# A decoder layer on one core: the first score maximum ahead of the root, next tokens normalized a slot ahead, cross keys at the slot's end, cross output ahead of the key sums

## The chip, the core and the metric

The kernel runs on one core of a Trainium2 chip. Its engines are TensorE (PE in the profile; PEld is its weight loads), VectorE (DVE), ScalarE (ACT), GpSimd (POOL) and SyncE (SP), which issues most of the transfers. Each engine takes its instructions in order, and waits at an instruction until the semaphores it names have been reached. The metric is device time in microseconds, the median of the runs. Before the change it is 855.12 us over 3 runs (855.03 to 855.3).

## What is computed

A pre-norm decoder layer in fp32 over 16 rows of 128 tokens with 256 features: self attention with 16 heads of 64, cross attention with 16 heads of 16 on a context of the same size under a mask that is the same for all rows, and a dense mixture of 8 experts whose sum is scaled per token.

```python
x = x + self_attention(layernorm(x))        # softmax(QK'/8) V, W_O, biases
x = x + cross_attention(layernorm(x), ctx)  # softmax(mask(QK'/4)) V, Wo, biases
x = x + moe(layernorm(x))                   # sum_e gelu(x w1_e + b1_e) w2_e + b2_e, scaled by norm_g

def self_attention(x):
    scores = einsum('bqhk,bshk->bhqs', Q, K) / sqrt(64)
    return einsum('bqhk,hdk->bqd', einsum('bhqs,bshk->bqhk', softmax(scores), V), W_O) + b_O
```

## The kernel before, in words

The program has two parts. The attention part handles one row of 128 tokens after the other, and the expert part follows it over all tokens. The change touches only the attention part, which takes roughly the first 450 us.

The attention part is a software pipeline of 16 slots. Slot s holds the self attention of row s, the cross scores of row s-1, the cross output of row s-2 and the last normalization of row s-3. It also makes queries, keys and values of later rows, two rows at a time, by a scheme with seven products in place of eight: `paired_steps` for queries (names `q...`) and keys (`k...`), and `paired_values` (names `v...`).

The order of instructions is written out by hand. Each step of a slot has a name, and the table `DUE` (L55) gives every name a due time in us from the slot's start. `slot` (L1027) puts the steps into a heap with the key `EXTRA + s * SLOT + due` (`when`, L307), and `run_slots` pops them in that order; each engine's queue has the order in which its instructions were popped. The due times are sort keys and nothing else: no instruction waits for a clock. `FIRST_DUE`, `SECOND_DUE` and `LAST_DUE` replace some times in slots 0, 1, 14 and 15. Names that end in `e` or that name a read-out (`vu0`, `qc1`, `at2T`, ...) are the copies or additions by which ScalarE or VectorE take a result out of PSUM; their due times are given apart from the matmuls'.

The steps that the text needs, with the engines in brackets:

- `S0`, `S1` (PE): self scores of heads 0 to 7 and 8 to 15 (`self_scores`), each into one of two score tiles (`ps_sc`, two banks of PSUM each).
- `max0`, `max1` (DVE, 128x1024): their negated maxima; `ex0a`, `ex0b`, `ex1a`, `ex1b` (ACT): four exponentials each; `r..` (DVE): reciprocals of the sums; `mul..` (POOL): scaling. With a `c` ahead (`cmax0`, `cex0a`, ...) the same for the cross scores.
- `T1a1`, `T1a2`, `T1b1`, `T1b2` (PE): four transposes each of the self probabilities; `T2..` of the cross probabilities of row s-2. Their read-outs (`T2b1e`, ...) are copies of 128x512: on ACT for `T1a`, `T1b` and `T2a`, on DVE for `T2b`.
- `q1x`, `q1y`, `q2x`, `q2y`, and the same with `k` and `v` (PE): products of the seven-product scheme. `..1x` and `..2x` work in one PSUM tile, `..1y` and `..2y` in a second. The first tile is last read by `qc00` (ACT). The second is read by `qu2`, `qu3`, `qc1` and `qc0` (DVE), and likewise for `k` and `v`.
- `root`, `xn`, `xn3` (DVE): inverse root of the variances and normalization (`normalize_outputs`). `xn1`, `LN1`, `LN1c` (DVE, PE, ACT): normalization and transposes of two new rows (`self_norm_transposed`, odd slots to 11, and slot 0). `LNx`, `LNxc`: the same for the cross queries' row; `LN3`, `LN3c` for the experts.
- `CQ`, `CS`, `CV`, `CO` (PE): cross queries, cross scores (into both score tiles), cross values, cross output. `ck`, `cke`, `cke2`: cross keys and their four read-outs on ACT. `cvr`, `cvre`: cross value rows.
- `msk0`, `msk1` (DVE): the mask. `SVa`, `SVb`, `atT0`, `atT1`: self values and their read-outs. `SO`, `xsSO`: self output.

All matmul results but the scores share the pool `ps_mm`, which has four tiles of one PSUM bank:

```python
ps_mm = tc.tile_pool(name="ps_mm", bufs=4, space=PSUM, side="right")
ps_sc = tc.tile_pool(name="ps_sc", bufs=2, space=PSUM)
```

A matmul that opens a tile waits for the last reader of the tile that was in that bank before.

Of the kernel before, what the change touches and what calls it, by code (L numbers as in the profile page):

```python
# [30 lines left out]
GB = 2  # L31
NG = B // GB
# [17 lines left out]
NROW = 528  # L50


SLOT = 26.98
EXTRA = 7.86
DUE = dict(  # L55
    S0=0.0, S1=1.0, T2a1=2.05, T2a2=2.49, T2a1e=2.69, ck=2.92, T2a2e=3.19, max0=3.47, v1x=3.79,
    cke=3.99, vu0=4.3, cke2=4.4, max1=4.61, v1y=4.66, q1x=5.52, ex0a=5.54, vu1=6.08, q1y=6.42,
    vu2=6.76, qu0=6.91, vu3=7.24, r0a=7.32, v2x=7.32, mul0a=7.39, vc00=7.4, ex0b=7.41, qu1=7.63,
    v2y=7.77, qu2=8.06, qu3=8.49, LNx=8.6, q2x=8.64, vc1=8.84, q2y=9.09, LNxc=9.1, ex1a=9.13,
    vc0=9.19, r0b=9.53, mul0b=9.81, qc1=10.19, cvr=10.21, qc00=10.51, qc0=10.54, r1a=10.98,  # L60
    T2b1=11.23, mul1a=11.26, cvre=11.31, ex1b=11.66, T2b2=11.66, T2b1e=11.86, CQ=12.1,
    T2b2e=12.46, T1a1=12.97, q2T=13.17, T1a2=13.4, r1b=13.51, xn1=13.6, T1a1e=13.6, mul1b=13.79,
    CS=13.93, st0=14.0, mid=14.0, late=14.0, T1a2e=14.1, ab1=14.9, CV=14.97, msk0=15.08,
    LN3=16.07, at2T=16.27, T1b1=16.29, LN3c=16.49, msk1=16.61, T1b2=16.73, T1b1e=16.93,
    LN1=17.16, T1b2e=17.43, SVa=17.47, cmax0=17.8, LN1c=17.93, SVb=18.38, tf=18.93, mid2=18.93,
    atT0=18.94, late2=18.94, cex0a=19.12, k1x=19.43, atT1=19.54, cmax1=20.14, k1y=20.33,
    cex0b=20.49, SO=21.23, cr0a=21.28, cmul0a=21.56, ku0=21.86, cr0b=22.14, cex1a=22.36,
    cmul0b=22.58, ku1=22.58, ku2=23.01, ku3=23.44, cex1b=23.74, cr1a=23.94, st1=24.0,
    cmul1a=24.3, k2x=24.68, xsSO=24.88, k2y=25.12, bn=25.28, kc00=25.32, cr1b=25.78, CO=26.03,
    cmul1b=26.06, kc1=26.22, kc0=26.57, xsCO=27.09, bn3=27.5, root=28.09, xn=34.27, ab2=34.3,  # L70
    xn3=37.78,
)


FIRST_DUE = dict(
    fk0=-11.4, fq0=-9.5, fk0e=-9.4, fq0e=-7.7, fk1=-7.2, norm1=-7.0, S0=-5.4, fk1e=-5.3,
    fq1=-4.4, max0=-4.0, cross=-3.0, ex0a=-2.7, fLN=-2.65, fq1e=-2.6, fv0=-2.3, fLNc=-1.4,
    r0a=-1.32, ex0b=-1.3, mul0a=-1.2, S1=-0.6, fv0e=0.1, r0b=0.15, mul0b=0.2, fab0=0.25,
    fab1=0.3, max1=0.4, fv1=0.41, ex1a=1.65, early0=1.7, early1=1.75, cvr=2.22, fv1e=3.0,
    r1a=3.1, mul1a=3.2, early2=3.3, early3=3.35, ex1b=3.6, q0=3.96, cvre=5.0, r1b=5.1,  # L80
    mul1b=5.2, q0e=5.3, early=5.4, k0=6.57, ke0=8.56, ws0=8.7, v0=9.18, xn1=10.44, T1a1=10.9,
    ve0=11.1, T1a2=11.34, T1a1e=11.54, T1b1=11.77, T1a2e=12.14, T1b2=12.21, LN1=12.64,
    T1b1e=12.74, LN1c=13.06, T1b2e=13.34, w0q=13.6, w0k=13.7, SVa=14.25, SVb=15.15, atT0=15.42,
    q1=17.2, atT1=17.21, wv0=17.3, q1e=17.6, k1=18.0, w1q=18.1, tf=18.2, SO=19.16, ke1=19.6,
    ws1=19.7, w1k=20.0, xsSO=22.81, bn=23.22, v1=23.47, root=24.79, xn=25.0, ck=25.2, ve1=25.39,
    q1x=26.9, cke=26.9, cke2=26.91, qu0=26.95, q1y=27.8, qu1=28.2, ab2=28.44, ab1=28.5,
    k1x=28.7, qu2=28.8, k1y=28.9, qu3=29.2, ku0=29.3, ku1=29.85, ku2=30.0, ku3=30.1, q2x=30.5,
    q2y=30.95, qc00=31.0, qc1=32.0, qc0=32.5, k2x=32.8, kc00=33.3, k2y=33.4, kc1=34.5, kc0=34.9,
# [2 lines left out]
SECOND_DUE = dict(wv1=4.7, st0=11.9, st1=12.46, st2=16.3, tf=19.6, st3=24.0)  # L91

LAST_DUE = {
    14: dict(root=30.48, xn=33.0),
    15: dict(
        max0=1.2, max1=2.35, ex0a=3.3, cke=4.6, cke2=4.65, r0a=5.2, mul0a=5.4, vu0=5.9, ex0b=6.0,
        LNx=7.24, qu1=7.4, cvr=7.46, LNxc=7.6, ex1a=8.0, r0b=8.3, T2b1=8.33, mul0b=8.5,
        T2b2=8.77, T2b1e=8.85, CQ=9.2, T2b2e=9.3, cvre=9.5, ex1b=9.6, r1a=10.0, T1a1=10.1,
        mul1a=10.11, q2T=10.25, T1a2=10.55, CS=11.0, r1b=11.75, mul1b=11.85, CV=12.1,
        LN3=13.05, T1b1=13.3, T1b2=13.75,  # L100
    ),
}

# [11 lines left out]
def decoder_layer(  # L115
# [53 lines left out]
    def psum_mm(name):  # L169
        return ps_mm.tile([P, 512], F32, tag="mm", name=name)  # L170
# [51 lines left out]
    def context(g):  # L222
        c = work.tile([P, KD, GT], F32, tag="ctx", name=f"ctx{g}")
        nc.sync.dma_start(out=c, in_=ctxT[g])
        return c

    contexts = {0: context(0)}
# [55 lines left out]
    def urgent():  # L283

        return tc.high_priority()
# [5 lines left out]
    def at(name, f, *a):  # L291


        if now[0] is None:
            f(*a)
        else:
            heapq.heappush(events, (when(name), next(count), now[0], f, a))

    def due(name, f, *a):

        if now[0] is None:
            with urgent():
                f(*a)
        else:
            at(name, f, *a)

    def when(name):  # L307
# [3 lines left out]
        if s == 1 and name in SECOND_DUE:  # L311
            return EXTRA + SLOT + SECOND_DUE[name]
        d = LAST_DUE[s] if s in LAST_DUE and name in LAST_DUE[s] else DUE
        return EXTRA + s * SLOT + d[name]

# [446 lines left out]
    def cross_keys(b):  # L762
        kT = work.tile([P, C2, 2, T], F32, tag="k2T", name="k2T")
        g, i = b // GB, b % GB
        mm = psum_mm("mm_k2")[:, : C2 * T].rearrange("p (m t) -> p m t", m=C2)
        for m in range(C2):
            for k in range(KD):
                nc.tensor.matmul(
                    mm[:, m, :],
                    wx[:, 1, k, m * P : (m + 1) * P],  # L770
                    contexts[g][:, k, i * T : (i + 1) * T],
                    start=(k == 0),
                    stop=(k == KD - 1),
                )


        def out(m):
            for e in range(2):
                nc.scalar.activation(
                    kT[:, m, e, :],  # L780
                    mm[:, m, :],
                    AF.Identity,
                    bias=bkp[:, e, m : m + 1],
                    scale=par[:, e : e + 1],
                )

        due("cke", out, 0)
        due("cke2", out, 1)
        entry["k2T", b] = kT

    def cross_value_rows(b):
        g, i = b // GB, b % GB
        mm = psum_mm("mm_v2")
        for k in range(KD):
            nc.tensor.matmul(
                mm[:, :D],
                contexts[g][:, k, i * T : (i + 1) * T],
                wx_vo[:, 0, k, :],
                start=(k == 0),
                stop=(k == KD - 1),  # L800
            )
        due(
            "cvre",
            nc.scalar.copy,
            v2s[g % 2][:, i].rearrange("p (e w) -> p e w", e=2)[:, :, :D].rearrange(
                "p e (r t) -> p e r t", t=32
            )[:, :, :, :DH2],
            mm[:, :D].rearrange("p (r e d) -> p e r d", e=2, d=DH2),
        )
        if i == GB - 1 and g + 2 < NG:  # L810
            contexts[g + 2] = context(g + 2)

    def cross_queries(b):
        xnT2 = entry.pop(("xnT2", b))
# [212 lines left out]
    def slot(s):  # L1027


        for half in range(2):  # L1030
            at(f"S{half}", self_scores, s, half)
            at(f"SV{'ab'[half]}", self_values, s, half)
            for n in range(2):
                at(f"T1{'ab'[half]}{n + 1}", self_transposed, s, half, n)
                if s >= 2:
                    at(f"T2{'ab'[half]}{n + 1}", cross_transposed, s - 2, half, n)
        at("SO", self_output, s)
        at("cvr", cross_value_rows, s)
        at("ck", cross_keys, s)
        normalize_outputs(s, s - 2 if s >= 2 else None)  # L1040
        if s >= 1:
            at("LNx", cross_norm, s - 1)
            at("CQ", cross_queries, s - 1)
            at("CS", cross_scores, s - 1)
            at("CS", cross_softmax, s - 1)
        if s >= 2:
            at("CV", cross_values, s - 2)
            at("CO", cross_output, s - 2)
        if s >= 3:
            at("LN3", expert_norm, s - 3)  # L1050
        bs = [2, 3] if s == 0 else [s + 3, s + 4] if s % 2 and s + 4 < B else []
# [3 lines left out]
        if bs:  # L1055
            at("LN1", self_norm_transposed, bs)
        b0 = s + 2 - s % 2
# [18 lines left out]
        if s >= B - 2:  # L1076
            at("S0", load_w1, s - (B - 2), we1)
        for n, (s1, name, out) in enumerate(PRE_STEPS):
# [466 lines left out]
```

## Time and profile before

| | |
|---|---|
| Median of the runs | 855.12 us |
| The profiled execution's own time | 856.78 us |
| Its span, first to last instruction | 855.0 us |
| Granted TensorE clock | 0.997 |
| PE, PEld busy | 99%, 84% |
| DVE, ACT, POOL busy | 75%, 56%, 19% |

Each row of a timeline has the start in us, the duration, the engine, the line, the operation, `out<-in` by the program's names, shapes, how many instructions were merged, and in brackets the idle time ahead of it with what ended it. fp32 matmuls appear as two passes each. Passes overlap, so busy time says little, and the distance from start to start says how fast TensorE goes on: 0.110 us for a pass with 128 columns, 0.216 for 256, 0.43 for 512.

The starts of slots (first score matmul, `sc<-kT,qT` at L706, from the chain of waits): slot 1 49.32, slot 2 73.69, slot 3 100.90, slot 4 128.34, slot 5 155.22, slot 6 182.66, slot 7 209.91, slot 8 237.23, slot 9 264.11, slot 10 291.43, slot 11 318.31, slot 12 345.63, slot 13 372.52, slot 14 399.40, slot 15 424.94. The chain merges rows, so that some of these starts lie up to 0.07 us behind the first matmul.

### The profile page before, as it was taken

The numbers are of one execution on the slowest core, as the hardware profiler recorded it, in microseconds if no ns is written. First come the engines' busy times: TensorE is split into PE (matmuls) and PEld (weight loads), VectorE is DVE, ScalarE is ACT, GpSimd is POOL, SyncE is SP. The second block draws the span as 40 slices with busy tenths as digits, with TensorE's granted clock in tenths as the row PEclk, the third lists the DMA queues.
The fourth block names the chain that finished last, engine by engine and source line by source line (L and its number), as shares of the span: only waits on it lengthen the run. The fifth ranks groups of instructions, "written<-read, shape, count | busy, mean of one in ns | idle before, by whom it ended". The sixth has DMA issues, their size and how long they took to land.

```text
span 855.0 us, 16389 instructions
## 1 busy us (share of the span) xinstructions
PE 846.0 (99%) x5934; PEld 721.8 (84%) x5934; DVE 642.2 (75%) x1694; ACT 474.6 (56%) x1723; POOL 164.7 (19%) x180
## 2 busy tenths in 40 slices
PE   8999999999999999999999999999999999999997
PEld 7899889888889889898775468888888888888886
DVE  4888998899888889888677497686557755676565
ACT  3567687776868668776685523343334333343332
POOL 4133242433423343332432000000000000000000
PEclk9999999999999999999999999999999999999999
DMA  8500000000000000001151100000000000000000
GB/s 238 148 13 2 2 14 2 15 1 2 13 2 14 1 2 14 2 2 51 56 196 46 50 1 0 1 13 13 1 0 1 26 1 0 1 13 13 2 0 26
DMA packets 18321, 21.32 MB, mean 25 GB/s; under 512 B 9584, under 2 KB 13696, under 8 KB 17600
## 3 DMA queue, kind: packets, MB, share of 16 engines
q1 hardware_dynamic: 17728, 19.93, 7.4%
q8 instruction: 47, 0.77, 0.4%
q0 software_dynamic: 368, 0.30, 0.2%
q14 instruction: 34, 0.28, 0.1%
q10 hardware_dynamic: 144, 0.04, 0.0%
HBM read 18.16 MB, written 2.10 MB: 24 GB/s over the span
## 4 chain that ended last, share of the span: by engine, by line
PE 93%; DVE 3%; ACT 2%; DMA 1%; issue 0%; POOLq 0%; DVEq 0%; SPq 0%; ACTq 0%
PE y L1279 20%; PE mm_qk L565 10%; PE tr_p L442 6%; PE mm_o L751 6%; PE he L1279 6%; PE hf L1279 6%; PE ha L1279 6%; PE mm_v L656 5%; PE sc L706 4%; PE po L731 3%; PE mm_h L1017 3%; PE hb L1279 3%; PE mm_qk L500 2%; PE y L1192 2%; PE po L880 2%; PE sc L841 2%
## 5 line engine op out<-in xcount | busy, mean ns | idle before, releaser
L412 ACT ACTIVATE cpr<-sc,nmax 128x128 f32<-128x128 f32 x256 | 90.5, 402 | 17.5 <-DVE nmax L406 14.0
L412 ACT ACTIVATE pr<-sc,nmax 128x128 f32<-128x128 f32 x256 | 93.0, 410 | 2.7 <-DVE nmax L406 2.7
L427 POOL TENSOR_TENSOR cpr<-cpr,rinv 128x512 f32<-128x512 f32 x64 | 65.5, 1040 | 126.4 <-DVE rinv L423 126.3
L1308 ACT ACTIVATE h<-u,colv 128x256 f32<-128x256 f32 x56 | 28.4, 508 | 99.4 <-DVE u L1295 97.5
L427 POOL TENSOR_TENSOR pr<-pr,rinv 128x512 f32<-128x512 f32 x64 | 67.1, 1049 | 62.8 <-DVE rinv L423 59.7
L406 DVE TENSOR_REDUCE nmax<-sc 128x8 f32<-128x1024 f32 x64 | 76.4, 1215 | 0.2 <-PE sc L706 0.2
L1309 DVE TENSOR_TENSOR c<-u,hf 128x256 f32<-128x256 f32 x56 | 23.5, 419 | 68.3 <-PE hf L1279 68.1
L1387 POOL TENSOR_TENSOR yT<-y,yu 128x256 f32<-128x256 f32 x1 | 0.7, 722 | 377.9 <-ACT y L1386 377.9
L1292 ACT COPY u<-ha 128x256 f32<-128x256 f32 x56 | 20.8, 372 | 83.5 <-PE ha L1279 83.5
L1279 PE MATMUL hf<-xt,w 128*128 128x256 f32 x224 | 66.7, 379 | 0.0
L1279 PE MATMUL ha<-xnT,w 128*128 128x256 f32 x224 | 66.6, 379 | 0.0
L1279 PE MATMUL y<-t,w 128*128 128x256 f32 x224 | 66.6, 380 | 0.0
L412 ACT ACTIVATION_READ_ACCUMULATOR pr<-sc,nmax 128x1 f32 x256 | 63.7, 249 | 0.0
L412 ACT ACTIVATION_READ_ACCUMULATOR cpr<-sc,nmax 128x1 f32 x256 | 61.9, 242 | 0.0
L751 PE MATMUL mm_o<-wo,atT 128*128 128x256 f32 x256 | 58.1, 380 | 0.3 <-DVE atT L324 0.3
L1279 PE MATMUL y<-h,w 128*128 128x256 f32 x224 | 57.6, 379 | 0.0
L751 PEld LDWEIGHTS mm_o<-wo,atT 128*128 128x128 f32 x256 | 47.6, 190 | 7.4 <-issue 1.0
L1279 PEld LDWEIGHTS ha<-xnT,w 128*128 128x128 f32 x224 | 42.6, 190 | 7.1 <-issue 1.2
L1279 PEld LDWEIGHTS hf<-xt,w 128*128 128x128 f32 x224 | 42.5, 190 | 5.9 <-DVE u L1294 0.2
L1279 PEld LDWEIGHTS y<-h,w 128*128 128x128 f32 x224 | 42.6, 190 | 5.8
L1279 PEld LDWEIGHTS y<-t,w 128*128 128x128 f32 x224 | 41.9, 190 | 6.2 <-issue 0.8
L395 POOL TENSOR_TENSOR xs<-xs,rowv 128x256 f32<-128x256 f32 x32 | 23.3, 740 | 115.2 <-DVE xn L382 115.2
(253 smaller groups left out, 2115.3 us busy)
## 6 DMA issues: line engine op xcount, KB each, us to landing
w<-in_w SPq DMA_DIRECT2D x8, 1024.0 KB, 5.2
ctx<-in_ctxT SPq DMA_DIRECT2D x8, 256.0 KB, 2.5
out_x<-ot SPq DMA_DIRECT2D x8, 256.0 KB, 2.1
xs<-in_x SPq DMA_DIRECT2D x3, 512.0 KB, 5.8
wk<-in_wk SPq DMA_DIRECT2D x2, 512.0 KB, 7.2
wq<-in_wq SPq DMA_DIRECT2D x2, 512.0 KB, 7.8
wv<-in_wv SPq DMA_DIRECT2D x2, 512.0 KB, 9.7
wo<-in_wo SPq DMA_DIRECT2D x1, 1024.0 KB, 7.7
```

Of the source, the lines that this page charges most:

```text
L406: nc.vector.tensor_reduce(w["nmax"], sc, AX.X, ALU.max, negate=True)
L412: nc.scalar.activation(w["pr"][:, i, :], sc[:, i, :], AF.Exp, bias=w["nmax"][:, i : i + 1], scale=1.0, accum_out=sums[:, j : j + 1],)
L427: nc.gpsimd.tensor_tensor(four, four, w["rinv", n].unsqueeze(2).broadcast_to([P, 4, T]), ALU.mult)
L442: nc.tensor.transpose(tr[:, j, :], w["pr"][:, 4 * n + j, :], ident)
L565: nc.tensor.matmul(out[:, q, :], paired[x, n][m - 1][:, q], paired[b0][m - 1], start=clears and q == 0, stop=True, skip_group_check=True,)
L656: nc.tensor.matmul(out, paired[b0][m - 1], paired["v", n][m - 1], start=clears, stop=True, skip_group_check=True,)
L706: nc.tensor.matmul(sc[:, j, c * T : (c + 1) * T], qT[r, c, :], kT[r, c, :], start=True, stop=True,)
L731: nc.tensor.matmul(po[j * DH1 : (j + 1) * DH1, c, :], v[:, h * DH1 : (h + 1) * DH1], prT[:, 4 * j + c, :], start=True, stop=True,)
L751: nc.tensor.matmul(mm[:, :D], atT[:, c, :], wo[:, c, :], start=(c == 0), stop=(c == C1 - 1))
L1017: nc.tensor.matmul(mm, w1q[p // (NP // QN)][:, i, k, p % (NP // QN)], xnT[:, k, :MT], start=(k == 0), stop=(k == KD - 1),)
L1279: nc.tensor.matmul(out, left[p // q][n - 1][:, p % q], rights[n - 1], **flags)
L1308: nc.scalar.activation(h[:, 1, 1], u[:, 3], AF.Gelu, bias=col(B1 + 2 * p + 1))
```

## The change

No instruction is added or removed. Only the due times change, and the place where the load of the next context is issued (with `cross_keys` in place of `cross_value_rows`, so that it follows the later of the two). The numbers of TensorE's changes between array shapes are the same in both programs, 118.

What this does to a middle slot's order:

| Engine | before | after |
|---|---|---|
| PE | S0 S1 T2a **ck** v1x v1y q1x q1y v2x v2y **LNx q2x** q2y **cvr T2b CQ** T1a CS CV LN3 T1b **(LN1)** SVa SVb k1x k1y SO k2x k2y **CO** | S0 S1 T2a v1x v1y q1x q1y v2x v2y **q2x LNx** q2y **CQ T2b** T1a **(LN1)** CS CV **cvr** T1b LN3 **CO** SVa SVb k1x k1y SO k2x k2y **ck** |
| DVE, first half | root **max0 max1** vu1 vu2 vu3 xn r0a qu1 qu2 qu3 **vc1 vc0** r0b qc1 qc0 xn3 .. T2b1e T2b2e q2T .. msk0 | **max0** root xn vu1 vu2 vu3 qu1 qu2 r0a qu3 **max1** xn3 r0b qc0 vc0 q2T T2b1e T2b2e r1b r1a **qc1** msk0 **vc1** at2T msk1 |
| DVE, second half | at2T msk1 cmax0 atT0 atT1 cmax1 .. | cmax0 cmax1 atT1 atT0 .. |
| ACT, first half | T2a1e T2a2e **cke** vu0 **cke2** ex0a qu0 .. | ex0a T2a1e vu0 T2a2e qu0 vc00 ex0b LNxc qc00 ex1b ex1a (LN1c) T1a1e T1a2e cvre .. **cke cke2** at the slot's end |

(LN1) stands in the slots that normalize two new rows. `xn1`, the normalization in front of it on DVE, moves to the slot before.

```diff
-SLOT = 26.98
+SLOT = 26.82
 EXTRA = 7.86
 DUE = dict(
-    S0=0.0, S1=1.0, T2a1=2.05, T2a2=2.49, T2a1e=2.69, ck=2.92, T2a2e=3.19, max0=3.47, v1x=3.79,
-    cke=3.99, vu0=4.3, cke2=4.4, max1=4.61, v1y=4.66, q1x=5.52, ex0a=5.54, vu1=6.08, q1y=6.42,
-    vu2=6.76, qu0=6.91, vu3=7.24, r0a=7.32, v2x=7.32, mul0a=7.39, vc00=7.4, ex0b=7.41, qu1=7.63,
-    v2y=7.77, qu2=8.06, qu3=8.49, LNx=8.6, q2x=8.64, vc1=8.84, q2y=9.09, LNxc=9.1, ex1a=9.13,
-    vc0=9.19, r0b=9.53, mul0b=9.81, qc1=10.19, cvr=10.21, qc00=10.51, qc0=10.54, r1a=10.98,
-    T2b1=11.23, mul1a=11.26, cvre=11.31, ex1b=11.66, T2b2=11.66, T2b1e=11.86, CQ=12.1,
-    T2b2e=12.46, T1a1=12.97, q2T=13.17, T1a2=13.4, r1b=13.51, xn1=13.6, T1a1e=13.6, mul1b=13.79,
-    CS=13.93, st0=14.0, mid=14.0, late=14.0, T1a2e=14.1, ab1=14.9, CV=14.97, msk0=15.08,
-    LN3=16.07, at2T=16.27, T1b1=16.29, LN3c=16.49, msk1=16.61, T1b2=16.73, T1b1e=16.93,
-    LN1=17.16, T1b2e=17.43, SVa=17.47, cmax0=17.8, LN1c=17.93, SVb=18.38, tf=18.93, mid2=18.93,
-    atT0=18.94, late2=18.94, cex0a=19.12, k1x=19.43, atT1=19.54, cmax1=20.14, k1y=20.33,
-    cex0b=20.49, SO=21.23, cr0a=21.28, cmul0a=21.56, ku0=21.86, cr0b=22.14, cex1a=22.36,
-    cmul0b=22.58, ku1=22.58, ku2=23.01, ku3=23.44, cex1b=23.74, cr1a=23.94, st1=24.0,
-    cmul1a=24.3, k2x=24.68, xsSO=24.88, k2y=25.12, bn=25.28, kc00=25.32, cr1b=25.78, CO=26.03,
-    cmul1b=26.06, kc1=26.22, kc0=26.57, xsCO=27.09, bn3=27.5, root=28.09, xn=34.27, ab2=34.3,
-    xn3=37.78,
+    xn1=-5.06, S0=0.0, S1=1.0, max0=1.2, T2a1=2.05, ab1=2.2, T2a2=2.49, ex0a=2.52, v1x=2.92,
+    v1y=3.79, T2a1e=3.89, vu0=4.39, q1x=4.65, T2a2e=4.74, vu1=5.19, q1y=5.55, vu2=5.62,
+    qu0=5.75, vu3=6.05, v2x=6.45, qu1=6.47, v2y=6.89, qu2=6.9, vc00=7.09, r0a=7.25, qu3=7.38,
+    ex0b=7.44, mul0a=7.53, max1=7.73, q2x=7.75, LNx=8.2, q2y=8.42, LNxc=8.81, qc00=9.11,
+    CQ=9.33, r0b=9.37, qc0=9.52, ex1b=9.61, mul0b=9.65, vc0=9.96, T2b1=10.2, q2T=10.4,
+    T2b2=10.63, T2b1e=10.83, ex1a=10.98, T1a1=11.07, T2b2e=11.43, T1a2=11.5, LN1=11.94,
+    r1b=12.03, CS=12.25, mul1b=12.31, LN1c=12.36, r1a=12.55, T1a1e=12.66, qc1=12.68,
+    T1a2e=13.16, CV=13.29, mul1a=13.33, msk0=13.4, cvr=14.39, vc1=14.59, at2T=14.94, T1b1=15.26,
+    msk1=15.28, cvre=15.46, T1b2=15.7, LN3=16.13, CO=16.35, cmax0=16.47, LN3c=16.55,
+    T1b1e=16.85, SVa=17.31, T1b2e=17.35, cmax1=17.61, cex0b=17.85, SVb=18.21, cex0a=19.23,
+    k1x=19.26, atT1=19.31, atT0=19.91, k1y=20.16, st0=20.51, mid=20.51, late=20.51, st1=20.52,
+    mid2=20.55, late2=20.55, ku0=20.6, tf=21.01, SO=21.06, cex1b=21.1, ku1=21.41, cex1a=22.47,
+    ku2=23.26, ku3=23.69, cr0a=24.04, cr1b=24.17, cr1a=24.3, cmul0a=24.32, xsCO=24.43,
+    k2x=24.51, xsSO=24.77, k2y=24.96, kc00=25.16, bn=25.18, cr0b=25.68, ck=25.86, cmul0b=25.96,
+    kc1=26.06, bn3=26.41, kc0=26.91, cke=26.93, cke2=26.98, cmul1b=26.98, cmul1a=28.0,
+    root=29.16, xn=31.51, xn3=35.69, ab2=37.49,
 )
...
 LAST_DUE = {
-    14: dict(root=30.48, xn=33.0),
+    14: dict(root=30.3, xn=32.7),
     15: dict(
-        max0=1.2, max1=2.35, ex0a=3.3, cke=4.6, cke2=4.65, r0a=5.2, mul0a=5.4, vu0=5.9, ex0b=6.0,
-        LNx=7.24, qu1=7.4, cvr=7.46, LNxc=7.6, ex1a=8.0, r0b=8.3, T2b1=8.33, mul0b=8.5,
-        T2b2=8.77, T2b1e=8.85, CQ=9.2, T2b2e=9.3, cvre=9.5, ex1b=9.6, r1a=10.0, T1a1=10.1,
-        mul1a=10.11, q2T=10.25, T1a2=10.55, CS=11.0, r1b=11.75, mul1b=11.85, CV=12.1,
-        LN3=13.05, T1b1=13.3, T1b2=13.75,
+        max0=1.2, max1=2.35, ex0a=2.5, T2a1e=3.89, T2a2e=4.4, ex0b=4.95, r0a=6.0, mul0a=6.05,
+        vu0=6.3, LNx=6.45, qu1=6.5, r0b=6.6, mul0b=6.65, T2b1=6.7, LNxc=6.75, ex1a=7.1,
+        T2b2=7.15, T2b1e=7.4, CQ=7.6, T2b2e=7.9, T1a1=8.5, ex1b=8.55, q2T=8.7, r1a=8.8,
+        mul1a=8.85, T1a2=8.95, CS=9.4, T1a1e=9.9, r1b=10.0, mul1b=10.05, T1a2e=10.4, CV=10.5,
+        cvr=11.5, T1b1=12.4, T1b2=12.85,
     ),
 }
...
         due("cke", out, 0)
         due("cke2", out, 1)
+        if i == GB - 1 and g + 2 < NG:
+            contexts[g + 2] = context(g + 2)
         entry["k2T", b] = kT
...
-        if i == GB - 1 and g + 2 < NG:
-            contexts[g + 2] = context(g + 2)
```

## The prediction, made before the changed kernel was run

> **What bounds the kernel now.** I read the page's busy shares first, then its chain of waits.
>
> ```profile
> PE 846.0 (99%) x5934; PEld 721.8 (84%) x5934; DVE 642.2 (75%) x1694; ACT 474.6 (56%) x1723; POOL 164.7 (19%) x180
> ...
> PE 93%; DVE 3%; ACT 2%; DMA 1%; issue 0%; POOLq 0%; DVEq 0%; SPq 0%; ACTq 0%
> ```
>
> TensorE is on the path 93% of the time, so any gain has to be a hole on TensorE. The timeline of one slot (128.27 to 155.15 us, 26.88 long; "+x" below is us after the slot's first score matmul) shows its holes. TensorE's rows:
>
> ```profile
> 137.10 0.61 PE L565 MATMUL mm_qk<-xnT,wq 128*128 128x128 f32 x4
> 137.67 0.71 PE L565 MATMUL mm_qk<-sums_v,wq 128*128 128x128 f32 x4
> 138.22 0.61 PE L565 MATMUL mm_qk<-xnT,sums_q 128*128 128x128 f32 x4
> ...
> 140.42 1.06 PE L819 MATMUL mm_q<-xnT,wx 128*128 128x128 f32 x8
> 141.31 1.04 PE L442 MATMUL tr_p<-ident,pr 128*128 128x128 f32 x8
> 142.28 1.15 PE L841 MATMUL sc<-k2T,q2T 32*128 32x256 f32 x16
> ```
>
> Starts count, not busy times: four passes of 128 columns take 0.45 (137.67+0.55=138.22 is the exception), eight take 0.89. The second row (`q2y`) should begin at 137.55; it begins at 137.67, and its second pass another 0.10 late. Hole: 0.23. What it waited for is on VectorE's timeline, with other rows that I need:
>
> ```profile
> 131.77 2.35 DVE L406 TENSOR_REDUCE nmax<-sc 128x8 f32<-128x1024 f32 x2
> ...
> 137.20 0.42 DVE L324 TENSOR_TENSOR qT<-su,mm_qk 128x256 f32<-128x256 f32 x1
> ...
> 140.17 1.29 DVE L324 COPY cprT<-tr_p 128x512 f32<-128x512 f32 x2
> 141.51 0.42 DVE L324 TENSOR_TENSOR q2T<-mm_q,bqk 128x256 f32<-128x256 f32 x1
> 141.96 0.18 DVE L423 RECIPROCAL rinv<-sums 128x4 f32<-128x4 f32 x1
> ```
>
> `qu3` ends at 137.62, so a matmul effectively flows 0.16 after the end it waits for (a transpose, by the same reading of LN1 at 172.47, 0.11). No other hole recurs. ScalarE:
>
> ```profile
> 131.00 1.07 ACT L324 COPY cprT<-tr_p 128x512 f32<-128x512 f32 x2 [3.76 <-PE tr_p L442]
> ...
> 141.29 0.47 ACT L412 ACTIVATE pr<-sc,nmax 128x128 f32<-128x128 f32 x1
> ```
>
> A PSUM copy of 512 columns is 0.59; the last exponential's start to its reciprocal is 141.96-141.29=0.67; four exponentials are 1.37.
>
> The Trainium skill ("Perfetto Trace Analysis", Identifying the Most-Contended Engine) says not to judge TensorE's headroom by matmul busy time but by LDWEIGHTS busy. That is 84% here: some 133 us of room. The starts give 0.23 per slot, about 3 us over slots 1 to 13. Page and trace differ, and I take the starts: they show each gap.
>
> **The change, part by part.** Engines issue the same instructions; only orders change. Mode switches of TensorE's array stay 118, so its dense slot is 26.88-0.23=26.65, with the four transposes of LN1 (0.44) 27.09. From the starts in that slot, the new order's dense steps are: S0 and S1 1.98, T2a 0.93, v1x 0.87, v1y 0.86, q1x 0.89, q1y 0.90, v2x 0.43, v2y 0.87, q2x 0.45, LNx 0.21, q2y 0.89, CQ 0.89, T2b 0.89, T1a 0.97, which puts CS at +12.03. The dense offsets below are their running sum.
>
> *First maximum ahead of the root.* `max0` runs at +1.17 (S1 starts at +0.99; the last pass of S0 ends 0.18 later) instead of +3.50, the root's 12 small operations (129.51 to 131.77: 2.26) after it, `xn` at +4.68, `vu1` +5.0, `qu3` +7.42 to +7.84. `q2y`, now behind LNx, is due at +8.39: its hole goes, -0.23 per slot. The large roots move behind `atT`: the holes before `SO` in slots 2 and 6 (0.54 and 0.31) go too. Exponentials start at +2.48 (1.17+1.22+0.09); the copy T2a1e behind four of them starts at +3.85 and ends at +4.44, and `q1x` (+4.64) needs +4.60: cover 0.04. LNxc stands behind `vc00` (+7.05, 0.27) and four exponentials (to +8.69) and ends at +9.08, `CQ` (+9.28) needs +9.24: cover 0.04.
>
> *Next tokens normalized ahead.* Two `xn` of 0.41 and two POOL additions of 0.73 leave the slot's middle for the slot before; POOL sat idle 7.36 there, so its queue hides them, and LN1's transposes can stand before CS. On VectorE they delay `ku2` by 0.8, with over 1 of cover in the middle slots.
>
> *Keys at the slot's end.* Eight passes (0.89) move. Four activations (1.4 on ScalarE) move from before the exponentials to where VectorE's maximum (to +2.39) hides them. The context load goes with them past nothing on SP; 256 KB land in 2.5 us and are wanted two slots later: free. In slot 15 the cover is gone: the four activations stand before the closing `cprT` copies, the third transposition waits for the first copy: +1.0.
>
> *Value rows behind CV, cross output before the key sums.* This removes what separated CQ, T2b, T1a and CS. Meanwhile `qc1` and `vc1`, the last readers of two PSUM banks, go from 10.19 and 8.84 to 12.68 and 14.59. There are four banks (`ps_mm`). Between +9.3 and +12.7 two are held, and CQ, T2b1, T2b2, T1a1, T1a2, LN1 take turns in the other two. In the built program T2b2 waits for `q2T`, T1a1 for T2b1e, T1a2 for T2b2e, LN1 for `qc1`. Working it out from the rows:
> - CQ +9.28, its result ready +10.34, `q2T` to +10.76 (0.42). T2b2 at +10.87, dense +10.61: hole 0.26.
> - T2b1 ready +10.78, VectorE copy 0.69, to +11.47. T1a1 +11.58, dense +11.31: 0.27.
> - T2b2 ready +11.47, copy to +12.13. T1a2 +12.24, dense +12.02: 0.22.
> - CS +12.77 instead of +12.03. It also waits for the last exponential: `max1` ends +8.97, eight from +9.44, last end +12.31. That alone allows +12.47.
> - `atT1`, now first, frees `k1y`'s bank: 0.05.
>
> Sum 0.80: slot 27.45 against 26.88, +0.57.
>
> With LN1 (odd slots to 11): `qc1` stands behind `r1a`, which needs the last exponential: 11.84+0.67=+12.51; `qc1` +12.63 to +13.05; LN1 +13.16, dense +12.68: another 0.5. Slot 28.4 against 27.32: +1.08.
>
> The skill's rule (same page, Optimizing Tensor Performance, Matmuls) that groups should rotate through different banks so that an evacuation overlaps the next group speaks against this. With four banks rotating, as now, the sum is 26.65 per slot; with two, by the 0.69 copies, 27.45. I take the latter, because the waits stand in the program.
>
> *The ends.* Slot 0: two `xn` (2x0.41) fall between `qu3` and `ku1`; `k2y` had 0.40 of cover: +0.5. Slot 1: LN1 waits for `qc1` (+12.1, dense +10.4: 1.8), T1a2 0.26, `SO` for `atT0`, which stands behind both cross maxima (2x1.15), `atT1` and the pair factors (+21.7, dense +19.5: 2.3); less today's holes, 24.37 becomes 27.6: +3.2. Slot 14: LNx and CQ stand together, without q2y between them, so CQ waits for the whole LNxc (transposes ready 0.17 after the last pass, copy 0.38, 0.16): 0.7; T1a2 0.1, CS for the exponentials 0.4: +1.2. Slot 15: `cvr` and `ck`, 1.75 together, leave their places ahead of CS, which comes to +9.35 while the sixteen exponentials end at about +10: a hole of 0.75 against 0.2 now, +0.55. Bounds where no row is close: `SO` in slot 1 from 0 (if the maxima find VectorE free 2 earlier) to 3, and I take 2.3 by the 1.15 pitch of two maxima; closing copies from 0 to the activations' whole 1.4, and I take 1.0, since the first copy starts only 0.69 after its transposes. A middle slot's hole goes from 0.44 (CS by the exponentials) to 0.95 (one more copy in the chain late).
>
> **Sum.** Slot 0 +0.5; 1 +3.2; 2 0 (27.21 to 27.2); 3, 5: +1.0 each, 7, 9, 11: +1.08 each, 5.2; 4, 8, 10, 12, 13: +0.57 each, 6: +0.2, 3.05; 14 +1.2; 15 and closing +1.55. Together +14.7 (0.5+3.2+5.2+3.05+1.2+1.55), on the profiled span of 855.0 (that execution's own time 856.78; median of the runs 855.12): 869.7 for the span, 869.8 for the median. The expert stage is unchanged.
>
> **Rivals.**
> - *The holes close and nothing opens.* For it: after `max0`, every wait up to CQ is met. 13x0.23=3.0: 852.1. Against: T2b2's wait follows CQ's own result. It would need the bank waits to be other than built. 6%.
> - *Only the exponentials bind.* If evacuations run beside TensorE, CS comes at +12.47, a hole 0.44 in place of 0.23 without LN1, nearly none with it (dense CS is +12.47): 7x0.21-5x0.23=0.3, plus slot 0 0.5, slot 1 2.0, slot 14 1.1 and slot 15 with the closing copies 1.55: +5.4, 860.5. For it: POOL and ScalarE are 19 and 56% busy. 8%.
> - *The two covers of 0.04 fail as well*: 0.1 to 0.15 each in 14 slots, +3.5: 873.3. For it: ScalarE's copies vary by 0.1. 17%.
> - *Nothing measurable* (within 0.2%, 1.7 us, about what a measurement of this kernel can tell from no change): gains and holes cancel, 855. 3%.
> - The forecast: 66%, own range 865 to 874.
>
> From this 861 to 876 leaves out the faster and the unchanged case and a little above. Faster 6%, same 3%, slower 91%.
>
> **What will show it.** In the timeline after: `q2y` 0.45 long; T2b2 0.7 after T2b1 rather than 0.44; the first `tr_p<-ident,pr` not 0.89 behind the `cpr` one but about 1.4; CS near +12.8, near +13.7 where four `tr_x` precede it; slots of 27.4 and 28.4. TensorE's idle put to VectorE. The prediction is wrong if CS comes at +12.1, or if slots 3 to 13 lose nothing and the loss lies at the ends.

## The result, and the profile after

The changed kernel takes 874.01 us (median of 4 runs, 873.58 to 875.94) against 855.17 of the kernel before on the same chip: a ratio of 1.0223, 95% interval 1.021 to 1.0235. It is slower by 18.8 us, and the forecast was 14.7. The profiled execution took 873.98 us; its span is 872.2 at a granted clock of 0.999, so the clock plays no part.

The page's busy shares and its chain of waits, after:

```profile
PE 853.6 (98%) x5934; PEld 719.9 (83%) x5934; DVE 639.0 (73%) x1694; ACT 476.4 (55%) x1723; POOL 163.3 (19%) x180
...
PE 84%; DVE 10%; issue 2%; ACT 2%; POOL 0%; DMA 0%; POOLq 0%; DVEq 0%; ACTq 0%
```

TensorE still counts as busy for 98% of the span and its weight loads for 83% (99% and 84% before), which would tell nothing. The chain tells it: TensorE's share fell from 93% to 84%, VectorE's rose from 3% to 10%. TensorE now often stands and waits for a VectorE result.

Where the time went, slot by slot (first score matmul to first score matmul, from the traces; the last row runs from slot 15's start to the expert part's first `y` matmul, L1192):

| Slots | before | after | change of each | forecast |
|---|---|---|---|---|
| 0 | 34.71 | 35.13 | +0.42 | +0.5 |
| 1 | 24.38 | 27.65 | +3.27 | +3.2 |
| 2 | 27.20 | 27.42 | +0.22 | 0 |
| 3, 5 | 27.44, 27.45 | 28.88, 28.77 | +1.44, +1.32 | +1.0 |
| 7, 9, 11 | 27.32 | 28.91, 28.77, 28.77 | +1.59, +1.45, +1.45 | +1.08 |
| 4, 8, 10, 12, 13 | 26.88 | 27.64 | +0.76 | +0.57 |
| 6 | 27.24 | 27.64 | +0.40 | +0.2 |
| 14 | 25.54 | 27.06 | +1.52 | +1.2 |
| 15 and closing | 49.19 | 51.13 | +1.94 | +1.55 |

The changes add up to 18.8, and the expert part behind them, to its last matmul, is equal within 0.02 us (376.33 and 376.31). So the whole loss lies in the slots. The spans differ by only 17.2, since this execution's slot 0 began 1.6 us earlier (12.93 against 14.54); the other runs' profiles began between 12.6 and 13.4.

The timeline of slot 4 (132.01 to 159.64), TensorE's rows that answer to those shown of before:

```profile
140.42 0.61 PE L565 MATMUL mm_qk<-sums_v,wq 128*128 128x128 f32 x4
140.86 0.61 PE L565 MATMUL mm_qk<-xnT,sums_q 128*128 128x128 f32 x4
141.31 1.06 PE L819 MATMUL mm_q<-xnT,wx 128*128 128x128 f32 x8
142.20 1.34 PE L442 MATMUL tr_p<-ident,cpr 128*128 128x128 f32 x8
143.68 1.36 PE L442 MATMUL tr_p<-ident,pr 128*128 128x128 f32 x8
144.97 1.15 PE L841 MATMUL sc<-k2T,q2T 32*128 32x256 f32 x16
```

`q2y` (the first two rows) is dense: 0.44 and 0.45. Up to `CQ` at +9.30 nothing waits. Then two groups of eight transposes, which need 0.89 and 0.97, take 1.48 and 1.29, and the cross scores start at +12.96 in place of the dense +12.03. The chain of waits for the same stretch says what releases each step (start, duration, engine, tile, line):

```profile
142.12 0.33 DVE v L324
142.45 0.39 DVE q2T L324
142.84 0.04 issue
142.88 0.67 PE tr_p L442 x4
143.55 0.03 issue
143.58 0.04 DVE cprT L324
143.61 0.57 issue
144.19 0.18 DVE rinv L423
144.37 0.05 issue
144.42 0.63 PE tr_p L442 x4
```

`q2T` ends at 142.83 and T2b2 starts at 142.88; T2b1's copy ends at 143.54 (both from VectorE's timeline) and T1a1 starts at 143.68; T2b2's copy ends at 144.27 and T1a2 starts at 144.42. These are the three tile waits of the forecast, one after the other. (Ahead of T1a2 the chain names a reciprocal, but TensorE's own semaphore instruction for VectorE ran from 144.31, 0.04 behind the copy, while that reciprocal went on until 144.36.)

Slot 5 holds something that was not forecast. VectorE's and GpSimd's rows beside two rows of TensorE:

```profile
161.99 0.53 DVE L370 TENSOR_SCALAR var<-mv 128x2 f32<-128x2 f32 x1
162.56 0.65 DVE L334 TENSOR_SCALAR root_t<-var 128x2 int32<-128x2 int32 x1
...
161.76 1.42 POOL L395 TENSOR_TENSOR xs<-xs,rowv 128x256 f32<-128x256 f32 x2
...
166.09 0.61 PE L656 MATMUL mm_v<-wv,xnT 128*128 128x256 f32 x2
166.99 0.70 PE L656 MATMUL mm_v<-wv,sums_v 128*128 128x256 f32 x2 [0.28 <-DVE v L324]
```

The first two operations of the root, 0.16 and 0.17 in slot 4, take 0.53 and 0.65 here, and each ends just after one of GpSimd's two additions. Everything behind them on VectorE is 0.85 late. `v2x` (the fourth row) goes on time, but `v2y` has to wait for a `v` read-out: 0.90 from start to start where 0.43 is dense.

### The profile page after: what moved, and what is told of

The parts are those of the page before. It is cut to its first block, busy times and chain, and to the rows that moved or that the text cites. A ratio compares the mean times of both kernels' runs of the same rounds, so it can differ in the third digit from the quotient of the medians.

```text
span 872.2 us, 16329 instructions
## 1 busy us (share of the span) xinstructions
PE 853.6 (98%) x5934; PEld 719.9 (83%) x5934; DVE 639.0 (73%) x1694; ACT 476.4 (55%) x1723; POOL 163.3 (19%) x180
## 4 chain that ended last, share of the span: by engine, by line
PE 84%; DVE 10%; issue 2%; ACT 2%; POOL 0%; DMA 0%; POOLq 0%; DVEq 0%; ACTq 0%
PE y L1279 19%; PE mm_qk L565 8%; PE mm_o L751 6%; PE he L1279 6%; PE hf L1279 5%; PE ha L1279 5%; PE tr_p L442 5%; PE po L731 3%; PE mm_v L656 3%; PE sc L706 3%; PE mm_h L1017 3%; PE hb L1279 3%; PE sc L841 2%; PE po L880 2%; PE mm_v L797 2%
## 5 line engine op out<-in xcount | busy, mean ns | idle before, releaser
L412 ACT ACTIVATE pr<-sc,nmax 128x128 f32<-128x128 f32 x256 | 91.0, 395 | 18.6 <-DVE nmax L406 9.5
L1308 ACT ACTIVATE h<-u,colv 128x256 f32<-128x256 f32 x56 | 28.4, 508 | 98.9 <-DVE u L1295 97.1
L412 ACT ACTIVATION_READ_ACCUMULATOR cpr<-sc,nmax 128x1 f32 x256 | 68.5, 268 | 0.0
L412 ACT ACTIVATION_READ_ACCUMULATOR pr<-sc,nmax 128x1 f32 x256 | 59.9, 234 | 0.0
L324 DVE COPY_PREDICATED_SCALAR sc<-hidden_keys,masked 128x1024 f32 x30 | 38.5, 1283 | 19.9 <-PE sc L841 19.9
```

The source lines that it names most:

```text
L412: nc.scalar.activation(w["pr"][:, i, :], sc[:, i, :], AF.Exp, bias=w["nmax"][:, i : i + 1], scale=1.0, accum_out=sums[:, j : j + 1],)
L1308: nc.scalar.activation(h[:, 1, 1], u[:, 3], AF.Gelu, bias=col(B1 + 2 * p + 1))
```

## The experiments

Twelve runs. Those on the changed kernel take back one part of it, or in the end three together; those on the kernel before do one part alone, or try another way to what the change wanted. Times are medians, ratios are to the kernel before on the same chip.

### The tiles given back, and held late

First the forecast's main cause by itself, in both directions. In the changed kernel, `qc1` and `vc1` ahead of `q2T`:

```diff
-    qc1=12.68, vc1=14.59,
+    qc1=9.98, vc1=10.0,
```

> The changed kernel with the last two read-outs of the second query and value tiles (qc1, vc1) put back ahead of q2T; nothing else. If two PSUM banks held too long make the middle slots long: the waits of T1a1 and T1a2 (0.30 and 0.27 in the slot from 132.01) go, T2b2 still waits about 0.25 (now for qc1), the cross scores come near +12.4 in place of +12.96, a part of it is given back at T1b, which then waits for GpSimd's last scaling; slots without LN1 27.64 to about 27.3, with LN1 28.8 to about 28.2, slot 1 27.65 to about 25.3; together some 6 us less (4 to 8) than the changed kernel's 874.0. If the exponentials or VectorE's own queue bind and the banks are incidental: the two additions ahead of q2T (0.8) only delay it, and the time stays within 1 us or grows.

864.74 us, ratio 1.0111 (1.0096 to 1.0126): 9.3 us of the 18.8 come back. TensorE's rows of its slot from 128.98:

```profile
139.18 1.35 PE L442 MATMUL tr_p<-ident,cpr 128*128 128x128 f32 x8
140.36 1.04 PE L442 MATMUL tr_p<-ident,pr 128*128 128x128 f32 x8
141.33 1.29 PE L841 MATMUL sc<-k2T,q2T 32*128 32x256 f32 x16
```

The second group starts 1.18 behind the first instead of 1.48, and takes 0.97, dense: T1a1 and T1a2 wait for nothing. T2b2's wait of 0.28 stays. The cross scores begin at +12.35. The slots are 27.17, 28.0 with LN1, and 25.82 for slot 1. That fits the first theory; two points of it are off. Nothing is given back at T1b, whose transposes run dense. And the cross scores themselves last 1.22 to the next step instead of 1.08: now ScalarE's exponentials bind. The read-out of the last exponential's sum is this row of ScalarE:

```profile
141.14 0.30 ACT L412 ACTIVATION_READ_ACCUMULATOR pr<-sc,nmax 128x1 f32 x1
```

It ends at 141.44, or +12.46. The first two score matmuls start at 141.33; the next two, which open the second score tile, start at 141.49, while in the kernel before all four start within 0.02. The forecast had the exponentials allow the cross scores at +12.47, so this limit was right, and the tile waits had covered it. In slot 1 the cross scores last even 1.66, and slot 1 is half a microsecond longer than the 25.3 that was expected; since `SO` waits for VectorE there as well, the runs don't tell how much of that is the exponentials'.

The converse, in the kernel before, whose order is otherwise untouched:

```diff
-    vc1=8.84, qc1=10.19,
+    vc1=14.59, qc1=12.7,
```

> The kernel before with qc1 and vc1 moved late (12.7 and 14.59 in place of 10.19 and 8.84) and nothing else. If banks held late are what costs: T2b1, T2b2 and CQ have to take turns in two banks, each waiting for the other's copy, 0.8 to 1.4 a slot in slots 3 to 13 and more at the start: 863 to 873. If it is the place of the cross queries and of the exponentials in the new order that costs, and not the banks: no change, within 1 us of 855.

873.82 us, ratio 1.0215 (1.0198 to 1.0232), just above the range of the first theory. Two read-outs moved late lose as much as the whole change, without any of its other parts. TensorE's rows in the slot from 130.68 (at L795 the cross value rows, then T2b, CQ, T1a):

```profile
141.02 1.03 PE L795 MATMUL mm_v<-wx_vo,ctx 128*128 128x256 f32 x4
142.74 1.06 PE L442 MATMUL tr_p<-ident,cpr 128*128 128x128 f32 x8 [0.69 <-ACT qT L576]
144.15 1.16 PE L819 MATMUL mm_q<-xnT,wx 128*128 128x128 f32 x8 [0.35 <-DVE cprT L324]
```

T2b waits for the read-out of another tile (`qc00` on ScalarE), and CQ for T2b1's copy: 1.72 and 1.41 from start to start where 0.87 and 0.89 are dense. Slots of 28.30 in place of 26.88. That this costs twice what giving the tiles back brought belongs to the old order, in which T2b also has to wait for `qc00`: the run shows the cause, and not the size it has in the new order.

How many free tiles does it take? The changed kernel with `vc1` alone put back:

```diff
-    vc1=14.59,
+    vc1=10.0,
```

> The changed kernel with only one of the two tiles given back: vc1 ahead of q2T, qc1 left where the change put it. If the number of free tiles is what counts: three turn in place of two, T1a1's wait (0.36) goes, T2b2 now waits for vc1, T1a2 and LN1 still wait for T2b's copies, and the gain is about half of that with both (9.3), 4 to 6: 868 to 870. If qc1 alone mattered, because LN1 waits for it: no gain outside slot 1, 872 or more. If one free tile were enough: 865.

865.56 us, ratio 1.0122 (1.0106 to 1.0137). The expectation of half the gain was wrong: one tile brings 8.5 of the 9.3, and its slots (27.15) are as short as with both. The chain of waits:

```profile
139.89 0.44 PE tr_p L442 x4
140.32 0.03 issue
140.36 1.65 PE tr_p L442 x12
142.01 1.05 PE sc L841 x13
```

With three tiles turning, a copy of 0.69 runs beside more than one group of 0.44 and is nearly covered; with two, each copy stands between two groups. That the middle slots come out equal is in part the exponentials' doing: the first score matmuls start at +12.41 here and at +12.35 with both tiles back, but those of the second score tile at +12.50 and +12.51. `qc1` alone was not tried.

### GpSimd beside VectorE's root

In the changed kernel, the two bias additions back where they were:

```diff
-    ab1=2.2,
+    ab1=14.9,
```

> The changed kernel with the two bias additions of GpSimd (ab1) put back from +2.2 to +14.9. If VectorE's root operations stall beside those additions (0.53 and 0.65 in place of 0.16 and 0.17 in the slot from 159.64) and so hold v2y back by 0.55: both rows return to 0.17 in the slots with LN1, the hole ahead of the second value matmul goes, LN1 then waits for qc1 instead, and these five slots become about 28.4 in place of 28.8: 2 us less in all. If the order of VectorE's steps alone makes that hole: nothing changes, within 0.5 us.

872.01 us, ratio 1.0202 (1.0187 to 1.0218): 2.0 us less. VectorE's rows at the same place:

```profile
161.43 0.16 DVE L370 TENSOR_SCALAR var<-mv 128x2 f32<-128x2 f32 x1
161.62 0.17 DVE L334 TENSOR_SCALAR root_t<-var 128x2 int32<-128x2 int32 x1
```

Both are short again, the hole ahead of `v2y` is gone, and the slots with LN1 are 28.35. There LN1 waits 0.25 for `qc1` (its read-out ends at 172.12, LN1 starts at 172.18), as the forecast said, though it had put 0.5; in the changed kernel most of that wait was hidden behind the other one. By the traces the five slots shorten by 0.41 to 0.56.

### The ends

In the changed kernel, three edits: in slot 1 (`SECOND_DUE`) `qc1` early and the `atT` read-outs ahead of the cross maxima, in slot 15 (`LAST_DUE`) one reciprocal and its scaling earlier:

```diff
 SECOND_DUE = dict(
...
+    qc1=9.98, atT0=16.46, atT1=16.45,
...
     15: dict(
...
+    cr0b=24.05, cmul0b=24.33,
```

> The changed kernel with three edits at its ends: in slot 1 qc1 ahead of q2T and atT0, atT1 ahead of the cross maxima, in slot 15 the reciprocal and scaling of the third group of cross probabilities (cr0b, cmul0b) ahead of the row's statistics. Slot 1: the waits of LN1 (1.6) and of SO (2.25) go, 27.65 to about 24.2. Closing: if the third transposition waits for GpSimd's scaling, which started late because its reciprocal stood behind the statistics, its hole of 1.49 goes; together 5 us less. If, as the prediction had it, the activations of the cross keys ahead of the copies hold it back, at least 1.0 of that hole stays; together 3.4 us less.

869.21 us, ratio 1.0164 (1.0149 to 1.0179): 4.8 less. Slot 1 is 24.22 in place of 27.65. Its two waits in the changed kernel stand in TensorE's timeline:

```profile
60.23 0.66 PE L391 MATMUL tr_x<-ident,xn 128*128 128x128 f32 x4 [1.43 <-DVE qT L324]
...
69.86 0.45 PE L751 MATMUL mm_o<-wo,atT 128*128 128x256 f32 x1 [2.08 <-DVE atT L324]
```

The stretch from slot 15's start to the expert part shrinks from 51.13 to 49.96. In the changed kernel the chain of waits there reads:

```profile
464.69 3.03 POOL cpr L427 x3
467.72 0.04 issue
467.76 1.09 PE tr_p L442 x8
```

TensorE waits for GpSimd: three scalings in a row, which could start only at 464.67 because the reciprocal of the first of them (464.45) stood on VectorE behind two additions and the statistics of a row:

```profile
464.45 0.14 DVE L423 RECIPROCAL rinv<-sums 128x4 f32<-128x4 f32 x1
```

With the reciprocal ahead, the transposes wait 0.23 in place of 1.49. The forecast's mechanism there (activations ahead of the copies) is refuted.

### All repairs together

> The changed kernel with the three repairs together: qc1 and vc1 ahead of q2T, ab1 at 14.9, and the edits at the ends. If the causes are separate and add up: 864.7 of the first alone, less 5 times 0.55 (the hole ahead of v2y; LN1 has no wait left to take it back), less 1.6 (the rest of slot 1), less 1.2 (closing): about 859. If one of them only hides another: 862 or more. It stays above 855 in both cases, since T2b2 still waits 0.3 in each slot and slots 14 and 15 keep their waits.

859.04 us, ratio 1.0043 (1.0028 to 1.0059), as expected. The middle slots are 27.17 and 27.46, slot 1 24.22. The three causes are separate but for slot 1, where the first and the third both give back the same 1.8, and they make up 15.0 of the 18.8. What is left lies in T2b2's wait, in the exponentials' 0.14 at the cross scores, and in slots 0, 14 and 15.

### What the change was after: the hole of q2y

The kernel before with the first maximum ahead of the root:

```diff
-    max0=3.47,
+    max0=1.05,
```

> The kernel before with the first maximum ahead of the root (max0 1.05 in place of 3.47) and nothing else. VectorE starts either of them at about +1.2 and has the same work up to qu3, and ScalarE's first exponentials stand behind the key activations, not behind the maximum. If ScalarE holds q2y: 855, within 0.5 us. If the place of the maximum closes q2y's hole, as the prediction had it: 852.

855.57 us, ratio 1.0004 (0.9995 to 1.0013), and every slot is within 0.01 of before. The hole is still there:

```profile
135.24 0.61 PE L565 MATMUL mm_qk<-xnT,wq 128*128 128x128 f32 x4
135.81 0.71 PE L565 MATMUL mm_qk<-sums_v,wq 128*128 128x128 f32 x4
```

The kernel before with the cross keys at the slot's end, nothing else:

```diff
-    ck=2.92, cke=3.99, cke2=4.4,
+    ck=26.06, cke=27.2, cke2=27.25,
```

> The kernel before with the cross keys and their four activations moved to the slot's end (ck 26.06, cke 27.2, cke2 27.25) and nothing else. If q2y's hole of 0.23 comes from ScalarE (qu0 stands behind the key activations and four exponentials, and VectorE waits for it): the activations leave, qu0 comes 1.5 earlier, the hole goes, and the kernel gains about 0.23 in 13 slots, 3 us: 852. If the hole comes from VectorE's order of root and maxima, as the prediction had it: no gain, and nothing above 1 us lost either way.

854.82 us, ratio 0.9993 (0.9985 to 1.0002). The hole did go, so ScalarE it was; but the 3 us did not come. TensorE's rows:

```profile
134.70 0.61 PE L565 MATMUL mm_qk<-xnT,wq 128*128 128x128 f32 x4
135.15 0.61 PE L565 MATMUL mm_qk<-sums_v,wq 128*128 128x128 f32 x4
...
136.91 1.05 PE L442 MATMUL tr_p<-ident,cpr 128*128 128x128 f32 x8
137.84 1.16 PE L819 MATMUL mm_q<-xnT,wx 128*128 128x128 f32 x8
```

`q2y` follows in 0.45, and CQ starts 0.93 behind T2b and loses another 0.10 at its second pass: it now waits for `qc00` (ScalarE, 137.35 to 137.78), which frees its tile. The slot is 26.80 in place of 26.88. One wait had covered the next.

Another way to bring ScalarE's `qu0` forward is to leave the keys and split the first four exponentials in two steps of two with `qu0` between them. The first try also moved the large roots, and the statistics `st0` with them, behind `atT` (the two steps' times in slots 0 and 15 are left out here):

```diff
-        def exponentials(n):
+        def exponentials(n, js=range(4)):
...
-            at(f"{x}ex{h}{q}", exponentials, n)
+            at(f"{x}ex{h}{q}", exponentials, n, range(2 if two and not n else 4))
+            if two and not n:
+                at("ex0a2", exponentials, n, (2, 3))
...
-    st0=14.0, mid=14.0, late=14.0, mid2=18.93, late2=18.93,
+    ex0a2=6.92, st0=20.51, mid=20.51, late=20.51, mid2=20.55, late2=20.55,
```

> The kernel before with two edits: the first four exponentials in two steps of two with qu0 between them (qu0 then starts when its products are there instead of 0.7 later), and the large roots (mid, late) behind atT. If ScalarE holds q2y and four tiles of PSUM keep turning: q2y's hole of 0.23 goes in 13 slots (3.0 us), the holes of 0.54 and 0.31 ahead of SO in slots 2 and 6 go: 851 to 852, below both kernels. If VectorE's order holds q2y, only the roots count: 854.3.

857.62 us, ratio 1.0027 (1.0017 to 1.0037): slower. The chain of waits in its slot from 126.71:

```profile
133.41 0.62 ACT su L576 x2
134.03 0.70 ACT pr L411 x4
134.74 0.03 issue
134.76 0.02 DVEq L422
134.78 0.04 issue
134.83 0.18 DVE rinv L422
135.01 0.32 DVE su L324
```

`qu0` (the first row) came early, but the reciprocal `r0a` stands ahead of `su` in VectorE's queue and needs the fourth exponential, which `qu0` had now pushed back. The roots at their new place held `su` of the keys, and slots 2 and 6 became longer too (27.45 and 27.49). With the roots and `st0` back, and with `r0a=8.55`, `mul0a=8.6`, behind `qu3`:

> The kernel before with the first four exponentials in two steps of two, qu0 between them, and the reciprocal r0a with its scaling mul0a behind qu3; the large roots stay where they are. In the run with the roots moved, r0a waited for the last of the four exponentials (134.83) and held su behind it on VectorE, which made q2y's hole 0.45 instead of 0.23. If that reciprocal is the new wait: with it out of the way qu3 comes over 1 us before q2y, the hole goes, the middle slots are 26.65 and 27.1 in place of 26.88 and 27.32, 3 us in all: 852. If splitting the exponentials itself costs (ScalarE's queue then binds CQ or the cross scores): 855 or more.

854.72 us, ratio 0.9991 (0.9982 to 1.0): the hole is gone and, as with the keys alone, CQ waits for `qc00`; 26.80 again. The run was expected to bring 3 us unless ScalarE's queue bound CQ; it does bind CQ, by 0.15 a slot.

So the keys at the end, with `qc00` moved ahead of the third four exponentials:

```diff
-    qc00=10.51,
+    qc00=9.12,
...
-    14: dict(root=30.48, xn=33.0),
+    14: dict(root=30.48, xn=33.0, qc00=10.51),
```

> The kernel before with the cross keys at the slot's end and, as a second edit, the read-out qc00 ahead of the third group of exponentials (9.12 in place of 10.51; in slot 14 it stays). With the keys alone q2y's hole went, and CQ waited for qc00 instead (0.04 and 0.10), since CQ takes the tile that qc00 frees. If that bank is the last wait in the slot: the even slots fall from 26.80 to 26.65, and the kernel to about 852.5 (13 times 0.14 below the 854.8 of the keys alone, and a little less in the first slots). If the exponentials, now 0.6 later, bind the cross scores: 854.5 to 856.

853.57 us, ratio 0.9977 (0.9968 to 0.9987). Even slots of 26.64, the dense length, and 27.08 with LN1 from slot 7 on. It falls short of 852.5 because slots 2, 3, 5 and 6 gain nothing: LN1 in slots 3 and 5 now waits 0.30 for `at2T`, and `SO` keeps its waits in slots 2 and 6. Two edits on VectorE deal with what is left in slots 2, 3, 5 and 6:

```diff
-    st0=14.0, mid2=18.93, late2=18.93,
+    st0=19.58, mid2=19.6, late2=19.6,
```

> The run with the keys at the slot's end and qc00 earlier, and two edits more on VectorE: the second half of the large roots (mid2, late2) from 18.93 to 19.6, behind both atT, and the statistics st0 from 14.0 to 19.58. If VectorE's statistics and roots make the waits left in slots 2, 3, 5 and 6 (LN1 waits 0.30 for at2T in slots 3 and 5; SO 0.54 and 0.31 in slots 2 and 6): these slots become 0.3 to 0.5 shorter each, about 1.4 in all, 852.2. If the root at its new place holds the second maximum and what follows it, as both halves did behind both maxima: no gain, 853.5 or more.

851.79 us, ratio 0.9962 (0.995 to 0.9975): faster than both kernels, 3.3 us below the one before, with slots of 26.60, 27.14, 27.08 and 26.93 at 2, 3, 5 and 6. The chain of waits on its page is back at TensorE's share of before, over a shorter span (850.5):

```profile
PE 93%; DVE 4%; ACT 1%; DMA 1%; issue 0%; POOLq 0%; DVEq 0%; SPq 0%; ACTq 0%
```

## Why the prediction was right, and where it was not

**Direction and cause** were right: a slower kernel, because `qc1` and `vc1` hold two of four tiles. It had worked that out from the program's waits, and two runs show it: giving the tiles back brings 9.3 us, and holding them in the old order costs 18.6. The rule of the Trainium skill that it set against the change ("Perfetto Trace Analysis", Optimizing Tensor Performance, Matmuls: groups rotating through different banks) is borne out: with two tiles the copies stand in the path, with three nearly none. The two covers of 0.04 were used up but held: in slots 4 and 5 `q1x` loses at most 0.02 and CQ nothing. So the rival that comes nearest in number (873.3, both covers failing) has the wrong mechanism, and 874.01 lies at the upper edge of the forecast's own range of 865 to 874. Slot 1 was right in both its terms (LN1 1.65 measured and 1.8 forecast, `SO` 2.3 and 2.3).

**The middle slot without LN1** was mis-sized by 0.19 (+0.76 in place of +0.57). From the starts, T2b2's hole is 0.24 (0.26 forecast), T1a1's 0.36 (0.27), T1a2's 0.30 (0.22). T2b2 starts at +10.87, just as forecast; the stops behind it were priced too low. The first copy ends at +11.53 in place of +11.47, because `q2T` stands ahead of it on VectorE until +10.82. T1a1 and T1a2 start 0.15 behind the copies that free their tiles, where the sum took 0.11. And T2b2's transposes, having waited, take 0.67 and not 0.60, so that the second copy comes later still.

**The slots with LN1** carried the largest error, 2.0 of 4.1 us. The step that failed is "two POOL additions of 0.73 leave the slot's middle for the slot before; POOL sat idle 7.36 there, so its queue hides them". GpSimd's queue was free, but VectorE was not indifferent to it: beside the additions its root took 0.85 longer. Putting `ab1` back brings 2.0 us. With it these slots are 28.35, and 28.4 was forecast; that is luck, since the middle slot's part of it was put 0.19 too low and LN1's wait 0.25 too high. The rule is in the Trainium skill ("SBUF — State Buffer", Who interferes with whom): GpSimd shares its SBUF ports with VectorE, and a `tensor_scalar` in a mode that needs both port pairs is shut out for the whole of GpSimd's instruction if that one began first. The trace agrees: 0.53 and 0.65 in place of 0.16 and 0.17, each ending 0.02 to 0.03 behind one of the additions; in which mode they ran no run here shows. An order table for each engine doesn't show such a conflict; it has to be looked for wherever work of GpSimd moves.

**What closed q2y's hole** was attributed wrongly: "first maximum ahead of the root ... its hole goes". The maximum alone changes nothing; the keys' activations leaving ScalarE did it. And the gain of 0.23 a slot would not have come whole: in the old order 0.15 of it reappears at CQ, as the runs with the keys alone and with the split show. Which of the moves closes it in the new order was not tested by itself.

**Closing copies**: +1.0 forecast with a bound of 1.4, 1.49 measured, by another mechanism. The forecast had the first copy behind four activations of the keys; the third transposition in fact waited for GpSimd's scaling, whose reciprocal had been moved behind the row's statistics. The forecast had checked ScalarE's queue and not VectorE's.

**Slot 14 and slot 15**. In slot 14 the terms are there: CQ waited 0.73 for LNxc (0.7 forecast), T1a2 0.19 (0.1), and the cross scores 0.25 for the exponentials (0.4): the last one's sum was read out until 426.82, and the second score tile was opened at 426.88. A matmul of the experts that lost 0.30 was not foreseen. In slot 15 the exponentials hold the cross scores for 0.69, as forecast (0.75). But they held them for 0.74 in the kernel before, where the forecast had put 0.2, so that this term came to nothing in place of +0.55. LNx, which was not forecast, waited 0.37. That the sum for slot 15 and the closing (1.55) came near 1.94 is therefore luck. The 0.42 of slot 0 was not tested.

## What to carry to other kernels

A read-out that nobody needs soon may still be urgent: it frees a bank. Count the free tiles between two steps before moving read-outs back; the step from two to three was worth 8.5 us here, that from three to four 0.8. And before pricing a hole that closes, ask what is late next: here q2y's 0.23 covered 0.15 at the following matmul, and only both moves together brought the slot to its dense 26.64.

## What the hardware showed that was not expected

Of VectorE's operations only `TENSOR_SCALAR` was slowed beside GpSimd. `xn` at L382 took 1.13 in place of 0.41 in 7 cases of the trace before, where it started while GpSimd worked. In the trace after, `var` took 0.46 to 0.65 and the root's first two steps (`root_t` at L334, `root` at L335) 0.64 to 0.96, in place of 0.16 and 0.17. Forms of 128x1 kept their 0.15 beside it. Maxima, reciprocals, statistics and the copies and additions that read PSUM kept their durations too. Since the long `xn` stand in the trace before, the conflict could have been read there ahead of the change.
